# Every fourth one-hot test of a list goes from VectorE to GpSimd

## The chip, the cores and the metric

The kernel runs on one NeuronCore of one Trainium2 chip. The metric is the device time of one execution in microseconds. Three runs of the kernel before gave 2284.84, 2287.78 and 2289.15 us; the median is 2287.78 us.

The core's engines are called by the profile PE (TensorE matmul), PEld (TensorE weight load), DVE (VectorE), ACT (ScalarE), POOL (GpSimd) and SP (SyncE, which here only issues DMAs).

## The reference

Four graph-attention layers run one after the other on 4096 nodes with 256 features each, over one adjacency matrix `adj` (4096 x 4096, int32) that all four share. It is sparse: about one entry in 256 is set, and the diagonal is always set. Cut to what matters:

```
for layer in 0..3:
    V  = x @ W                                   # 4, 4, 2, 1 heads
    e[i, j]  = leaky_relu(s1[i] + s2[j])         # per head
    att = softmax over j of (e where adj[i, j] else -inf)
    out = att @ V           # layer 3: also a negative attention, then fc and elu
    x = layernorm(x + out)
```

Because so few entries of a row of `adj` are set, 128 rows of it together touch only about four in ten of the columns. The kernel makes use of this.

## The kernel before

**Lists.** The 4096 nodes are 32 tiles of 128. For each tile `m` of 128 target nodes, the kernel makes a list of the source nodes that any of the 128 targets is connected to. It has room for 13 x 128 entries beside the tile's own 128 nodes, 14 positions of 128 in all. With the list goes a packed mask `cm` of 128 targets by 14 x 128 entries, and `idx`, the node numbers of the entries. `lists` (L288) is a generator with 36 steps. Its `prepare` (L370) reads a part of `adj` by DMA (`raw`, 512 KB each, L378), turns it into bytes on ACT (`mk`, L380) and finds on DVE which source nodes are hit (L384). `places` (L389) computes with matmuls the place of each hit node in its list. `pack` (L422) does the packing for one tile `m`.

**The one-hot tests.** `pack` goes through the 31 other source tiles `j` in order. For each it knows at build time a window of 1, 2 or 3 positions into which the nodes of tile `j` can fall. One instruction, L436, compares a row of numbers (`iota`, float16) with the place of each of the 128 source nodes (a [128, 1] operand), and leaves a one-hot matrix `oh` (bfloat16, 128 x 128, 256 or 384). One matmul for each position of the window (L442) then multiplies it with the bytes of the adjacency tile and adds the product into a PSUM bank. When the last tile that touches a bank is done, ACT copies the bank to `cm` (L449). At the end `cm` is stored to memory (L450) and `idx` is computed on DVE (L453 to L455). Over all 32 lists there are 992 tests and 2336 matmuls of L442. The buffers of `oh` come from a pool of 8.

```
oh = ohp.tile([P, WMAX], BF16, name="oh")
nc.vector.tensor_scalar(oh[:, :n * P], iota[:, :n * P], self.place[:, it, j:j + 1], None,
                        op0=ALU.is_equal)
```

**A layer.** For each row tile, `RowTile.load` (L619) gathers the rows of V and of the score terms of the listed nodes from memory: 13 indirect DMAs that GpSimd issues (L634), and one plain DMA for the tile's own nodes (L631). They land in slots `G`, two positions to a slot in layers 0 to 2. Layer 0 has 16 slots, and a row tile needs 7. `half` (L638) does seven of the 14 positions at a time: ACT computes exp(S + d) for three heads (L687, 128 x 128 each); for the fourth head DVE multiplies exponentials (L678, L682); DVE masks each head's 128 x 896 weights (L684 and L688); PE multiplies the weights with the gathered values (L696; L699 in layers 2 and 3). In layers 0 and 1 the mask is first copied into PSUM (L653), so that L684 and L688 read one input from SBUF and one from PSUM.

**Stages and order.** `run` (L482) mixes the lists into layer 0. First the projections of layer 0 run together with the first 14 steps of `lists`. Then in layer 0's loop over row tiles, `part(m, 0)` issues the gathers of tile m + 1 and the first half of tile m, the next step of `lists` (tile m + 10, `LEAD`) follows, and then `part(m, 1)`:

```
for m in range(NT):
    layer.part(m, 0)
    if m + LEAD < NT:
        next(lists)
    layer.part(m, 1)
```

The instructions are not left in this order: a scheduler of the framework reorders them when the program is built, by this order as priority and by its own estimate of when each can run. What it decides is fixed: on the chip each engine works through its own queue in order. In the profile the tests of L436 run from 57.6 to 663.0 us. Layers 1 to 3 use the lists without any further test. In those, L938 (with L927, L928, L935) treats the last row tiles of layers 2 and 3 without a list.

Of the kernel before, what the change touches and what calls it, by code (L numbers as in the profile page):

```python
# [39 lines left out]
BF16 = mybir.dt.bfloat16  # L40
# [5 lines left out]
ALU = mybir.AluOpType  # L46
# [4 lines left out]
P = 128  # L51
# [77 lines left out]
WMAX = max(n for _, n in WINDOW.values()) * P  # L129
# [59 lines left out]
class Program:  # L189
# [98 lines left out]
    def lists(self, ctx):  # L288


        tc, nc, ins, shared = self.tc, self.nc, self.ins, self.shared

        def pool(name, bufs):
            return ctx.enter_context(tc.tile_pool(name=name, bufs=bufs))

        cst, rawp, mkp, ohp = pool("icst", 1), pool("raw", 4), pool("imk", 2), pool("oh", 8)
# [5 lines left out]
        iota = cst.tile([P, WMAX], F16, name="iota")  # L302
# [41 lines left out]
        for j in range(NT):  # L344
            m = 0
            while m < NT:
# [6 lines left out]
                a, n = WINDOW[m, j]  # L353
# [10 lines left out]
        class Block:  # L364
# [57 lines left out]
            def pack(self, it):  # L422
                m, mk = self.blk * BT + it, self.mk
                cm = cmp_.tile([P, NP, MC], U8, name="cm")
                nc.scalar.copy(cm[:, FRONT, :], mk[:, m, it, :])
                order = [j for j in range(NT) if j != m]
                touches = {}
                for j in order:
                    a, n = WINDOW[m, j]
                    for k in range(a, a + n):  # L430
                        touches.setdefault(k // 3, []).append((j, k))
                accs = {}
                for j in order:
                    a, n = WINDOW[m, j]
                    oh = ohp.tile([P, WMAX], BF16, name="oh")
                    nc.vector.tensor_scalar(oh[:, :n * P], iota[:, :n * P], self.place[:, it, j:j + 1], None,  # L436
                                            op0=ALU.is_equal)
                    for k in range(a, a + n):
                        b, s = divmod(k, 3)
                        if b not in accs:  # L440
                            accs[b] = prog.bank(prog.pthree)
                        nc.tensor.matmul(accs[b][:, s * MC:(s + 1) * MC], oh[:, (k - a) * P:(k - a + 1) * P],  # L442
                                         mk[:, j, it, :].bitcast(FP8), start=touches[b][0] == (j, k),
                                         stop=touches[b][-1] == (j, k), skip_group_check=True)
                        if touches[b][-1] == (j, k):
                            e = min(3, NG - 3 * b)
                            got = accs[b][:, :e * MC].rearrange("p (s c) -> p s c", c=MC)
                            o = 3 * b + (3 * b >= FRONT)
                            nc.scalar.activation(cm[:, o:o + e, :], got, AF.Copy, scale=EDGE / 2.0)  # L449
                nc.sync.dma_start(out=shared["maskC"][m], in_=cm)  # L450

                t = wk.tile([P, NP], F32, name="t")
                nc.vector.scalar_tensor_tensor(t, cm[:, :, P], 16.0, cm[:, :, P + 1], op0=ALU.mult, op1=ALU.add)  # L453
                nc.vector.scalar_tensor_tensor(t, t, 16.0, cm[:, :, P + 2], op0=ALU.mult, op1=ALU.add)
                nc.vector.tensor_tensor(shared["idx"][:, m, :], t, limit, op=ALU.min)  # L455
# [1034 lines left out]
```

## Time and profile before

| | |
|---|---|
| median of 3 runs | 2287.78 us |
| the profiled execution, its own time | 2288.18 us |
| its span, first to last instruction | 2286.4 us |
| granted TensorE clock, mean | 0.961 |
| busy: PE, PEld, DVE, ACT, POOL | 2026.1, 1835.8, 1798.3, 1741.5, 1493.2 us |
| one-hot tests, L436 | 992, from 57.6 to 663.0 us, 225.7 us busy |
| gathers on GpSimd, L634 | 1456, 1480.2 us busy |

The page gives for each engine its busy time, its share of the span and its instructions, and further down the groups of instructions by line with busy time, the mean duration of one in ns, and the idle time just before them with what ended it. Durations of neighbouring DVE instructions overlap in the records: the 992 tests have a mean of 304 ns, but together they cover only 225.7 us, 228 ns each. A table of stretches gives busy time by engine between two moments. The list of waits tells who waited for whom.

### The profile page before, as it was taken

How to read it: one execution, taken by the hardware profiler on the slowest of the kernel's cores; microseconds unless marked ns; L12 is line 12 of the kernel's file. 1: busy time of each engine (PE TensorE's matmuls, PEld its weight loads, DVE VectorE, ACT ScalarE, POOL GpSimd, SP SyncE). 2: the span in 40 equal slices, each digit the busy share in tenths (PEclk: the TensorE clock that was granted, in tenths of full speed). 3: DMA queues.
4: the chain of work that ended last, by engine and by line, in shares of the span. 5: the costliest groups of instructions: out<-in, count | busy, mean ns of one | idle time of the engine just before them, and what ended most of it. 6: DMA issues, size and time to landing. Idle time of an engine off the chain costs nothing.

```text
span 2286.4 us, 49074 instructions
## 1 busy us (share of the span) xinstructions
PE 2026.1 (89%) x15689; PEld 1835.8 (80%) x15689; DVE 1798.3 (79%) x5317; ACT 1741.5 (76%) x4977; POOL 1493.2 (65%) x1596
## 2 busy tenths in 40 slices
PE   4888888988999968998889898989998799999996
PEld 2667877877889958998888887989997688888885
DVE  2898998989999968998888895887885365566566
ACT  4778887977789958988788886988883666676664
POOL 2117664646567777777777777777761677777773
PEclk7999999999999989999999999999999899999998
DMA  8889777866456765666666666778764788888884
GB/s 279 257 262 349 219 231 250 282 201 212 143 155 188 208 181 158 190 182 165 177 170 172 176 168 176 221 213 233 217 201 139 243 268 274 270 259 282 261 255 139
DMA packets 250320, 493.00 MB, mean 216 GB/s; under 512 B 44385, under 2 KB 156610, under 8 KB 249666
## 3 DMA queue, kind: packets, MB, share of 16 engines
q0 software_dynamic: 81536, 245.30, 38.0%
q1 hardware_dynamic: 168514, 244.46, 33.5%
q8 instruction: 126, 2.06, 0.4%
q14 instruction: 144, 1.18, 0.2%
HBM read 437.05 MB, written 52.54 MB: 214 GB/s over the span
## 4 chain that ended last, share of the span: by engine, by line
PE 51%; DVE 15%; DMA 14%; ACT 11%; issue 5%; POOL 3%; SPq 0%; DVEq 0%; ACTq 0%; POOLq 0%
PE bank L699 16%; PE bank L696 14%; PE bank L938 10%; DMA G<-vals,idx 8%; ACT w L687 6%; PE bank L550 5%; PE bank L442 4%; POOL G L634 3%; DVE w L688 3%; DMA raw<-in_adjB_dram 2%; DVE w L684 2%; DVE oh L436 2%; DVE w L678 1%; DMA G<-vals 1%; ACT mk L380 1%
## 5 line engine op out<-in xcount | busy, mean ns | idle before, releaser
L634 POOL DMA_INDIRECT G<-vals,idx x1456 | 1480.2, 1017 | 754.2 <-issue 205.0
L687 ACT ACTIVATE w<-S,G 128x128 f32<-128x128 f32 x3248 | 988.2, 389 | 122.9 <-DMA G<-vals,idx 106.8
L696 PE MATMUL bank<-w,G 128*65 128x128 f32 x7168 | 842.9, 277 | 102.0 <-DVE w L684 79.0
L696 PEld LDWEIGHTS bank<-w,G 128*65 128x65 f32 x7168 | 800.6, 140 | 120.8 <-DVE w L684 91.3
L699 PE MATMUL bank<-G,w 128*128 128x257 f32 (+1 forms) x2688 | 491.3, 340 | 33.6 <-DVE w L666 11.8
L699 PEld LDWEIGHTS bank<-G,w 128*128 128x128 f32 x2688 | 431.8, 193 | 83.5 <-DVE w L666 14.7
L688 DVE SCALAR_TENSOR_TENSOR w<-w,bank 128x896 f32<-128x896 f32 x384 | 411.7, 1081 | 21.0 <-ACT w L687 20.5
L938 PE MATMUL bank<-vw,pw 128*128 128x129 f32 (+1 forms) x2048 | 301.2, 304 | 6.6 <-issue 3.2
L938 PEld LDWEIGHTS bank<-vw,pw 128*128 128x128 f32 x2048 | 276.9, 193 | 23.7 <-issue 3.7
L664 ACT ACTIVATE w<-S,G 128x128 f32<-128x128 f32 x392 | 140.0, 391 | 128.7 <-DMA G<-vals 64.3
L436 DVE TENSOR_SCALAR oh<-iota,place 128x256 bf16<-128x256 f16 (+2 forms) x992 | 225.7, 304 | 14.7 <-PE bank L442 14.1
L442 PE MATMUL bank<-mk,oh 128*128 128x132 fp8e4 x2336 | 188.5, 224 | 18.1 <-DVE oh L436 9.2
L550 PE MATMUL bank<-wext,xT 128*128 128x268 f32 (+3 forms) x640 | 181.5, 415 | 16.4 <-ACT xT L541 14.4
L678 DVE TENSOR_TENSOR w<-S,G 128x256 f32<-128x256 f32 x384 | 154.4, 418 | 51.8 <-DMA G<-vals,idx 48.9
L442 PEld LDWEIGHTS <-oh 128*128 128x128 bf16 x2336 | 144.2, 98 | 58.8 <-DVE oh L436 27.3
L380 ACT ACTIVATE mk<-raw 128x1024 uint8<-128x1024 int32 x128 | 130.7, 1053 | 25.8 <-DMA raw<-in_adjB_dram 25.7
L550 PEld LDWEIGHTS bank<-wext,xT 128*128 128x128 f32 x640 | 118.4, 203 | 35.6 <-ACT xT L541 16.9
L927 ACT ACTIVATE pw<-Sw,d 128x512 f32<-128x512 f32 x192 | 131.6, 714 | 17.0 <-PE bank L938 12.7
L935 DVE TENSOR_TENSOR pw<-pw,mw 128x512 f32<-128x512 f32 x64 | 44.0, 692 | 124.3 <-ACT pw L934 65.6
L928 DVE SCALAR_TENSOR_TENSOR pw<-pw,mw 128x512 f32<-128x512 f32 x192 | 126.9, 692 | 18.2 <-ACT pw L927 17.4
L684 DVE SCALAR_TENSOR_TENSOR w<-w,bank 128x896 f32<-128x896 f32 x128 | 138.7, 1083 | 0.9
L688 DVE SCALAR_TENSOR_TENSOR w<-w,mk 128x896 f32<-128x896 f32 x80 | 86.7, 1087 | 43.1 <-ACT w L687 42.0
(131 smaller groups left out, 1605.0 us busy)
## 6 DMA issues: line engine op xcount, KB each, us to landing
raw<-in_adjB_dram SPq DMA_DIRECT2D x128, 512.0 KB
mk<-maskC SPq DMA_DIRECT2D x112, 231.0 KB
G<-vals,idx POOLq DMA_INDIRECT x1456
S<-edge SPq DMA_DIRECT2D x64, 256.0 KB
vw<-vals SPq DMA_DIRECT2D x96, 129.0 KB
xp<-y SPq DMA_DIRECT2D x96, 128.0 KB
y<-xp SPq DMA_DIRECT2D x96, 128.0 KB
mw<-maskW SPq DMA_DIRECT2D x20, 528.0 KB
```

Source lines behind the costliest of these rows:

```text
L380: nc.scalar.activation(mk[:, q:q + 2, :, :P], src, AF.Copy, scale=EDGE)
L436: nc.vector.tensor_scalar(oh[:, :n * P], iota[:, :n * P], self.place[:, it, j:j + 1], None, op0=ALU.is_equal)
L442: nc.tensor.matmul(accs[b][:, s * MC:(s + 1) * MC], oh[:, (k - a) * P:(k - a + 1) * P], mk[:, j, it, :].bitcast(FP8), start=touches[b][0] ...
L550: nc.tensor.matmul(pp[:, :c1 - c0], self.xT[:, k, :], wext[:, k, c0:c1], start=(k == 0), stop=(k == KT - 1 and brow is None))
L634: nc.gpsimd.indirect_dma_start(out=self.place(pos), out_offset=None, in_=sh["v"][n][:NODES[t], :], in_offset=bass.IndirectOffsetOnAxis(ap= ...
L678: nc.vector.tensor_tensor(w[h][:, k:k + 2, :], S[:, h:h + 1, :].to_broadcast([P, 2, P]), dd[:, :, V + T + h:V + T + h + 1].to_broadcast([P ...
L684: nc.vector.scalar_tensor_tensor(w[h], w[h], LEAST, mh, op0=ALU.max, op1=ALU.mult)
L687: nc.scalar.activation(w[h][:, k, :], S[:, h, :], AF.Exp, bias=d(k, h))
L688: nc.vector.scalar_tensor_tensor(w[h], w[h], LEAST, mh, op0=ALU.max, op1=ALU.mult)
L696: nc.tensor.matmul(accs[0][:Wd, h * P:(h + 1) * P], v, w[h][:, k, :], **how)
L699: nc.tensor.matmul(a, w[h][:, k, :], v, **how)
L938: nc.tensor.matmul(accs[it][:, c:c + Wd], p[:, it, :], v[:, c:c + Wd], start=(j == 0 and h == heads[0]), stop=(j == NT - 1), skip_group_ch ...
```

## The change

In `pack`, every test with `j % 4 == 3` is issued on GpSimd instead of VectorE. It writes to buffers of a name of its own, `ohg`, of which there are 4. The other tests stay on VectorE with their 8 buffers. The operation, its operands and the matmuls that read the result are the same.

```diff
-                    oh = ohp.tile([P, WMAX], BF16, name="oh")
-                    nc.vector.tensor_scalar(oh[:, :n * P], iota[:, :n * P], self.place[:, it, j:j + 1], None,
-                                            op0=ALU.is_equal)
+                    side = j % 4 == 3
+                    oh = ohp.tile([P, WMAX], BF16, name="ohg" if side else "oh", bufs=4 if side else None)
+                    (nc.gpsimd if side else nc.vector).tensor_scalar(oh[:, :n * P], iota[:, :n * P],
+                                                                     self.place[:, it, j:j + 1], None, op0=ALU.is_equal)
```

## The prediction

> **What bounds the kernel now.** I read first the table of busy time by stretches, cut at the first test (57 us), at the first weights of layer 0 (175 us) and at the last test (about 665 us), then the groups by line, then the waits in the middle stretch, then the order of time.
>
> ```profile
> core 0: us, PE busy (x) PEld busy (x) DVE busy (x) ACT busy (x) POOL busy (x), PEclk, DMA share, GB/s
> 57.00:175.00 118.00, 99.77 (x956) 76.63 (x957) 104.73 (x454) 87.30 (x220) 16.35 (x17) 0.92 0.84 263
> 175.00:665.00 490.00, 428.64 (x4190) 387.84 (x4187) 457.49 (x1432) 402.02 (x1191) 290.15 (x291) 0.96 0.72 229
> ```
>
> The second stretch, lists beside layer 0, lasts 490 us for 22 row tiles: 22.3 us each. DVE is the busiest engine (457.49 of 490, 93%), PE follows (87%), POOL has 290. In the first stretch DVE (89%), PE (85%) and DMA (84%) are all near the limit and POOL is nearly idle.
>
> ```profile
> L436 DVE TENSOR_SCALAR oh<-iota,place 128x256 bf16<-128x256 f16 (+2 forms) x992 | 225.7, 304 | 14.7 <-PE bank L442 14.1
> L634 POOL DMA_INDIRECT G<-vals,idx x1456 | 1480.2, 1017 | 754.2 <-issue 205.0
> ```
>
> The tests cover 225.7 us of DVE, 0.2275 us each. By size they take 252, 296 and 321 ns for 128, 256 and 384 elements: 0.27 ns for one more element, where the masking of L688 takes 1081 ns for 896, 1.2 ns each. [...]
>
> ```profile
> POOL G L634 <- PE bank L696: 83.7, 44, 10.5
> PEld L442 <- DVE oh L436: 17.4, 39, 2.0
> PE bank L442 <- DVE oh L436: 7.1, 10, 1.7
> ```
>
> These are waits in the second stretch: who waited for whom, us, times, the longest. POOL's queue stands still 83.7 us because a slot `G` isn't free until PE has read it. PE waits little for tests.
>
> ```profile
> 409.35 4.91 DVE L436 TENSOR_SCALAR oh<-iota,place 128x384 bf16<-128x384 f16 x22
> 409.48 0.99 POOL L634 DMA_INDIRECT G<-vals,idx  x1 [0.30 <-issue]
> 410.78 1.11 POOL L634 DMA_INDIRECT G<-vals,idx  x1 [0.30 <-ACT cm L449]
> 412.20 1.10 POOL L634 DMA_INDIRECT G<-vals,idx  x1 [0.30 <-ACT cm L449]
> 413.61 0.98 POOL L634 DMA_INDIRECT G<-vals,idx  x1 [0.30 <-issue]
> ```
>
> The order of time of one row tile: most tests of a list come in one run (22 in 4.91 us), some earlier in twos to fives between other work. At the same time POOL issues a row tile's 13 gathers back to back (398.02 to 414.59 us, 16.6 us), one each 1.25 us, and stands idle some 4.5 to 10 us until the next row's slots are free. Beside the run of tests a gather takes 1.1 us instead of the usual 0.95.
>
> [...]
>
> **The change, step by step.**
>
> *Removed from DVE.* Of the 31 tiles of a list, 8 have j % 4 = 3 (7 where m is one of them): 24 x 8 + 8 x 7 = 248 tests. At 0.2275 us that is 56.4 us of DVE: of the 321 tests before 175 us a quarter, 80 tests, 18 us; of the 671 after it 168 tests, 38 us.
>
> *Added to POOL.* The windows of the moved tests come to 31 x 128, 124 x 256 and 93 x 384, a mean of 288 elements. The nearest rows are POOL's affine selects, also a compare over one input:
>
> ```profile
> L319 POOL TENSOR_SCALAR_AFFINE_SELECT tri<-ones 128x128 bf16<-128x128 bf16 x1 | 0.3, 287 | 0.0
> L325 POOL TENSOR_SCALAR_AFFINE_SELECT tot<-ones 128x4 bf16<-128x4 bf16 x1 | 0.2, 184 | 0.0
> ```
>
> That is 0.83 ns an element on 0.18 us. Lower end: 0.18 + 288 x 0.83 ns = 0.42 us. [...] I take 0.55 us. Eight a row: 4.4 us on a POOL that has 16.6 of 22.3 us occupied: 21.0 us, so it fits, though barely, and stops fitting at (22.3 - 16.6) / 8 = 0.71 us.
>
> *The lock, on DVE's side.* [...] Mean 0.345 us, against the 0.2275 us saved: a loss of 0.12 us a test, 168 x 0.12 = 20 us of DVE time. With DVE at 93% I let three quarters through: +15 us. [...]
> In the first stretch tests are most of DVE's work (84 us in all three forms)[...], a loss of 0.20 x 80 = 16 us. There half is hidden by the loading of `raw` and by PE: +8 us. [...]
>
> *The new waits.* A moved test waits for one of 4 buffers, that is for an earlier L442 on PE, and for `place`, done a block ahead. Behind it on POOL's queue are the gathers of the next row; those who wait for them are L678 on DVE and L687 on ACT. The gathers that begin at 398 us serve weights that DVE begins at 418 us (first half, whose six gathers are issued by 405) and 428 us (second half, all issued by 414.6), with some 3 us to land: about 10 us of cover on each, and 4.4 us of tests fit under it. I charge nothing; without that cover each row would lose up to 4.4 us. The other way round, a moved test stands behind gathers: PE works in order and needs test j = 19, 23, 27, 31 in the middle of the run; alternating with gathers the last four take 4 x (1.25 + 0.55) = 7.2 us instead of the 4.91 us of the run. Behind the waiting L442 stand L696 and the projections. The list is ten row tiles ahead and the scheduler can put other matmuls between, so I charge a tenth of 2.3 x 22 us: +5 us, with 0 and +50 as ends. Nothing moves on SP, and no DMA is added or taken away.
>
> Sum: +15 + 8 + 5 = +28 us against the profiled execution's 2288.18 us (span 2286.4; 0.4 us over the median of the runs): 2316 us.
>
> **The rivals.**
>
> *Faster: the offload simply works.* POOL makes its tests in its idle time under maskings, the lock costs next to nothing, and DVE loses 38 us in the second stretch, from 457 to 419. Then PE (429) is late next: with the 32 us now left over DVE's busy time the stretch is 429 + 32 = 461 us, -29 us; in the first stretch the way from 105 to PE's 100 gives -5 us. 2254 us. For it: DVE is the busiest, POOL has a fourth to spare, the maskings are long. Against it: lock and run. It decides at a mean lock cost of 0.2275 us a test. With a half-way lock the gain is 5 to 20 us. Chance of any gain over 0.2%: 0.29.
>
> *Same.* The lock gives back what the move saved, and lists are ahead enough for the rest: 2288 us. Chance 0.11.
>
> *Slower by far: POOL becomes the bound.* If a test takes 1 us, POOL needs 16.6 + 8 = 24.6 us a row, 2.3 us over the period; after the first 10 us of cover this is 2.3 x 22 - 10 = +41 us[...]: about 2288 + 75 = 2363 us. Chance 0.15.
>
> That the change doesn't do what it says isn't likely: the diff leaves no other engine to take the tests.
>
> **How the numbers follow.** My forecast, a moderate loss of some 5 to 55 us, has 0.45; POOL-bound 0.15; same 0.11; gain 0.29. About 0.2% (4.6 us) is what a measurement of this kernel can tell from no change. So slower 0.60, same 0.11, faster 0.29. The range: the low end of 2260 us leaves out only the fullest form of the gain (about one in ten), the high end of 2372 us the worst of the POOL-bound case (one in ten). The likeliest case alone reaches from 2293 to 2343 us.
>
> **What would show it.** L436 on DVE with 744 tests and on POOL with 248; [...]DVE's remaining tests and L678 longer, or with gaps, where POOL has a test; DVE's busy and idle time together in the second stretch not down by 38 us; waits of PE L442 for POOL above DVE's 24 us of before; after 700 us nothing changed. The prediction is wrong if the second stretch gets shorter than 485 us, or if POOL's tests last over 0.71 us and gathers become what ends ACT's and DVE's waits there.

## The result, and the profile after

The changed kernel takes 2427.14 us (median of 4 runs, 2424.33 to 2429.73) against 2288.47 us of the kernel before, measured beside it: a ratio of 1.0612, 95% interval 1.0591 to 1.0632, or +139 us. The forecast was 2316 us with a range up to 2372 us: the sign was right, the size was not. The lines of code stand one lower than before: the test is L437, its matmul L443, the gather L635, the weighted matmul L697.

First the table of stretches of the changed kernel, cut at the same times as before, with one stretch more because the last test now ends at 797.5 us:

```profile
core 0: us, PE busy (x) PEld busy (x) DVE busy (x) ACT busy (x) POOL busy (x), PEclk, DMA share, GB/s
...
57.00:175.00 118.00, 93.97 (x871) 69.39 (x871) 97.94 (x341) 76.75 (x192) 86.53 (x84) 0.87 0.70 221
175.00:665.00 490.00, 352.26 (x3292) 334.95 (x3293) 349.01 (x989) 328.81 (x951) 375.37 (x372) 0.85 0.62 203
665.00:800.00 135.00, 101.22 (x979) 97.81 (x978) 101.57 (x307) 82.52 (x269) 99.88 (x101) 0.88 0.46 135
```

In the 490 us in the middle DVE is now busy for 349 where it was 457, and PE for 352 where it was 429. POOL comes nearest to its limit: it is busy for 375, and about 0.3 us pass ahead of each of the 237 gathers in it, so some 446 of the 490 us are taken. Yet it isn't full either. The last test ends 134.5 us later than before (797.5 against 663.0), and from there to the end the kernel takes 1630 us where it took 1623. The loss lies where the lists are made.

The costliest groups, from the page of the changed kernel:

```profile
L635 POOL DMA_INDIRECT G<-vals,idx x1456 | 1486.0, 1021 | 559.9 <-issue 211.1
...
L437 POOL TENSOR_SCALAR ohg<-iota,place 128x256 bf16<-128x256 f16 (+2 forms) x248 | 252.4, 1031 | 75.6 <-DVE place L411 59.5
...
L437 DVE TENSOR_SCALAR oh<-iota,place 128x256 bf16<-128x256 f16 (+2 forms) x744 | 197.3, 339 | 77.6 <-PE bank L443 77.1
...
L443 PE MATMUL bank<-mk,ohg 128*128 128x132 fp8e4 x558 | 87.5, 252 | 165.3 <-POOL ohg L437 164.5
```

The counts are those of the forecast, 248 and 744. A test on POOL takes 1.03 us, almost twice what was assumed. The last line is the one to look at: ahead of the matmuls that use POOL's tests PE stood idle for 165 us, and POOL is named as the cause. The waits from 175 to 800 us, with total, times and longest in us, say the same, and one thing more:

```profile
PEld L443 <- POOL ohg L437: 167.0, 37, 14.2
PE bank L443 <- POOL ohg L437: 159.2, 33, 14.0
DVE oh L437 <- PE bank L443: 72.4, 14, 11.0
...
POOL G L635 <- PE bank L697: 33.3, 39, 3.7
```

PE waits for POOL, about 5 us at a time (159.2 us in 33 waits); DVE waits for PE, which has to read a test before its buffer is free (72.4 us); and POOL waits for PE (33.3 us). (Of POOL's 39 waits for L697 most are the 0.3 us that pass ahead of any gather, and ten are 2 us or more.) Two engines that wait for each other are the sign of a loop. The order of time shows it (start, duration, engine, line; in brackets idle time before and who ended it):

```profile
473.77 1.22 POOL L635 DMA_INDIRECT G<-vals,idx  x1 [0.16 <-ACT w L688]
...
489.02 0.63 PE L443 MATMUL bank<-mk,oh 128*128 128x132 fp8e4 x8
...
493.20 0.94 POOL L635 DMA_INDIRECT G<-vals,idx  x1 [0.30 <-issue]
494.17 8.19 POOL L437 TENSOR_SCALAR ohg<-iota,place 128x384 bf16<-128x384 f16 x8
...
495.50 0.51 PE L443 MATMUL bank<-mk,ohg 128*128 128x132 fp8e4 x3 [5.85 <-POOL ohg L437]
...
498.78 7.38 PE L697 MATMUL bank<-w,G 128*65 128x128 f32 x56
...
505.13 1.03 POOL L635 DMA_INDIRECT G<-vals,idx  x1 [2.77 <-PE bank L697]
```

POOL issues 15 gathers here, two more than a row has (473.77 to 494.14 us, 20.4 us with one test among them). Only then comes its run of 8 tests: the last four of one list and the first four of the next, since there are four buffers. PE is done with what it has at 489.65 and stands until the first of these tests is there (495.50, 5.85 us). Behind that matmul on PE's queue stands the next half of L697. The first of its masked weights were there at 486.79 (end of L685), 2.9 us before PE stood still, and yet it starts only at 498.78, after the last of L443: PE keeps to the order of its queue. It is this half that frees the slots `G`, and POOL's next gathers wait for that until 505.13. From gather burst to gather burst that is 20.4 + 1.3 (one test) + 3.3 (the rest of the list) + 6.4 (into L697) = 31.4 us for 15 gathers. POOL itself is taken up for 28.6 of them and stands still for the last 2.8. On average, between 300 and 600 us, POOL issues 141 gathers, 27.7 us for 13; in the kernel before it issued 167, 23.4 us for 13. So two things are in the longer row: the tests on POOL take time of their own, and POOL and PE wait for each other.

### The profile page after: what moved, and what is told of

Same layout as the page of the kernel before. It is cut to its first block, busy times and chain, and to the rows that moved or that the text cites. A ratio compares the mean times of both kernels' runs of the same rounds, so it can differ in the third digit from the quotient of the medians.

```text
span 2427.9 us, 49044 instructions
## 1 busy us (share of the span) xinstructions
PE 2059.6 (85%) x15689; PEld 1887.7 (78%) x15689; DVE 1782.3 (73%) x5069; ACT 1738.8 (72%) x4977; POOL 1751.4 (72%) x1844
## 3 DMA queue, kind: packets, MB, share of 16 engines
q0 software_dynamic: 81536, 245.30, 35.3%
## 5 line engine op out<-in xcount | busy, mean ns | idle before, releaser
L635 POOL DMA_INDIRECT G<-vals,idx x1456 | 1486.0, 1021 | 559.9 <-issue 211.1
L697 PE MATMUL bank<-w,G 128*65 128x128 f32 x7168 | 846.9, 280 | 60.9 <-DVE w L685 48.1
L697 PEld LDWEIGHTS bank<-w,G 128*65 128x65 f32 x7168 | 817.9, 143 | 72.3 <-DVE w L685 57.0
L689 DVE SCALAR_TENSOR_TENSOR w<-w,bank 128x896 f32<-128x896 f32 x384 | 409.1, 1078 | 20.5 <-ACT w L688 20.0
L437 POOL TENSOR_SCALAR ohg<-iota,place 128x256 bf16<-128x256 f16 (+2 forms) x248 | 252.4, 1031 | 75.6 <-DVE place L411 59.5
L437 DVE TENSOR_SCALAR oh<-iota,place 128x256 bf16<-128x256 f16 (+2 forms) x744 | 197.3, 339 | 77.6 <-PE bank L443 77.1
L443 PE MATMUL bank<-mk,ohg 128*128 128x132 fp8e4 x558 | 87.5, 252 | 165.3 <-POOL ohg L437 164.5
L450 ACT ACTIVATE cm<-bank 128x396 uint8<-128x396 f32 (+1 forms) x160 | 68.7, 451 | 210.8 <-PE bank L443 210.8
L443 PE MATMUL bank<-mk,oh 128*128 128x132 fp8e4 x1778 | 184.6, 248 | 13.1 <-DVE oh L437 11.1
L679 DVE TENSOR_TENSOR w<-S,G 128x256 f32<-128x256 f32 x384 | 157.4, 426 | 49.9 <-DMA G<-vals,idx 47.9
L443 PEld LDWEIGHTS <-ohg 128*128 128x128 bf16 x558 | 48.0, 111 | 173.9 <-POOL ohg L437 173.5
L443 PEld LDWEIGHTS <-oh 128*128 128x128 bf16 x1778 | 138.1, 112 | 32.4 <-DVE oh L437 24.1
```

What stands on the lines that cost most here:

```text
L437: (nc.gpsimd if side else nc.vector).tensor_scalar(oh[:, :n * P], iota[:, :n * P], self.place[:, it, j:j + 1], None, op0=ALU.is_equal)
L635: nc.gpsimd.indirect_dma_start(out=self.place(pos), out_offset=None, in_=sh["v"][n][:NODES[t], :], in_offset=bass.IndirectOffsetOnAxis(ap= ...
L679: nc.vector.tensor_tensor(w[h][:, k:k + 2, :], S[:, h:h + 1, :].to_broadcast([P, 2, P]), dd[:, :, V + T + h:V + T + h + 1].to_broadcast([P ...
L689: nc.vector.scalar_tensor_tensor(w[h], w[h], LEAST, mh, op0=ALU.max, op1=ALU.mult)
L697: nc.tensor.matmul(accs[0][:Wd, h * P:(h + 1) * P], v, w[h][:, k, :], **how)
```

## The experiments

**Theory A, the loop**: POOL's tests stand behind the gathers, PE's matmuls behind the tests, the gathers behind PE's matmuls. **Theory B, POOL's own time**: 13 gathers and 8 tests of 1.03 us don't fit into 22.3 us. **Theory C, the slowing** (the recorded texts say "lock"): DVE's tests get longer while POOL has a test. By what means they would, no run shows. The three were taken apart one by one.

**Eight buffers instead of four (e1_bufs8).** All 8 tests of a list can then be made ahead of the gathers.

```
-oh = ohp.tile([P, WMAX], BF16, name="ohg" if side else "oh", bufs=4 if side else None)
+oh = ohp.tile([P, WMAX], BF16, name="ohg" if side else "oh", bufs=8 if side else None)
```

> The change with 8 ohg buffers in place of 4, so that GpSimd can make all tests of a list one row tile ahead. Theory A, queue order (PE stands because the last four tests of a list lie behind the 13 gathers of the next row tile, and only four fit ahead): PE's 164 us of waits for ohg fall below 40 us and the time comes back to 2290 to 2320 us. Theory B, GpSimd's own time (16.6 us of gathers and 8.2 us of tests against a row of 22.3 us): whatever the order, a row lasts 24.8 us or more, so the time stays at 2340 us or above, and the waits move to the gathers. Theory C[...]: no difference from the change as it is, 2427 us.

Measured: 2364.1 us, ratio to before 1.0321 (1.0292 to 1.0350); 63 us less than the changed kernel. That fits B (2340 us or more), not A alone (2290 to 2320 us). POOL's own order of time in this run:

```profile
474.79 8.92 POOL L437 TENSOR_SCALAR ohg<-iota,place 128x256 bf16<-128x256 f16 x8
483.87 1.03 POOL L635 DMA_INDIRECT G<-vals,idx  x1 [0.17 <-PE bank L443]
...
499.98 0.95 POOL L635 DMA_INDIRECT G<-vals,idx  x1 [0.30 <-issue]
500.96 8.53 POOL L437 TENSOR_SCALAR ohg<-iota,place 128x256 bf16<-128x256 f16 x8
```

From run to run of tests it is 26.2 us: 8.9 us of tests and 17.1 us of 13 gathers (25.3 us on average between 300 and 600 us). From 175 to 740 us POOL pauses for longer than the 0.3 us ahead of a gather only once (1.2 us). The loop is gone and POOL sets the pace: B. PE still waits for POOL, now the slowest engine (from 175 to 730 us):

```profile
PE bank L443 <- POOL ohg L437: 66.1, 46, 9.0
```

**The moved tests left out (e4_leave_out).** What is the relief of DVE worth without any cost? The kernel makes no test where j % 4 = 3, and their matmuls read one tile of zeros, so the lists lack those nodes.

```
+if j % 4 == 3:
+    oh = none
+else:
     oh = ohp.tile([P, WMAX], BF16, name="oh")
     nc.vector.tensor_scalar(oh[:, :n * P], ...)
```

> The 248 tests with j % 4 = 3 are left out altogether (their matmuls read one tile of zeros, so the entries of these source tiles are missing from the lists); GpSimd makes none. This is what the relief of VectorE is worth if GpSimd cost nothing. If VectorE sets the pace of the list stage: 56 us of its time gone, 34 us or more off, about 2254 us. If PE, the gathers or the loads set it as much: 2270 to 2288 us.

Measured: 2232.35 us, ratio 0.9743 (0.9713 to 0.9773), -58 us for 248 tests of 0.2275 us, which are 56.4 us. DVE's time counts in full. PE, at 429 of the 490 us from 175 to 665 us before, does 458 in this run (granted clock 0.99 there, 0.96 before), so it does not hold DVE's relief back. The gathers move as many bytes as before (245.30 MB), so lighter transfers are not the cause. The group of DVE's tests:

```profile
L441 DVE TENSOR_SCALAR oh<-iota,place 128x256 bf16<-128x256 f16 (+2 forms) x744 | 174.8, 301 | 7.1 <-PE bank L447 6.6
```

**Room on POOL (e6_plain_change, and e7_plain_before as its control).** In layer 0, eight of a row's 13 gathers are made plain copies of some rows by SP, in the changed kernel and in the kernel before alike. They bring other rows than the list names. POOL then has ample time for tests, and no long burst stands ahead of them; what is left is relief and slowing.

```
     ...
+    if n == 0 and t % 3:
+        nc.sync.dma_start(out=self.place(pos), in_=sh["v"][n][t * P:(t + 1) * P, :])
+        continue
     ...
```

> The change, with 8 of the 13 gathers of each row tile of layer 0 replaced by plain copies of 128 rows in order, issued by SP (same bytes, other rows, so layer 0's values differ): GpSimd's row falls to 5 gathers and 8 tests, 6.3 + 8.2 = 14.5 us, far under any row. To be held against e7, which has the same copies without the change. Theory that queue order and GpSimd's time are all there is: the difference to e7 is the worth of the relief found by leaving the tests out, -58 us. [...](0.2 to 0.35 us of VectorE for each test on GpSimd, as the longer tests of e1 and e3 suggest): 50 to 85 us of VectorE come back, difference -10 to +30 us.

> The kernel before with the same 8 gathers of a row tile of layer 0 as plain copies on SP: the control for e6. GpSimd was not what set the pace of the kernel before, so all theories expect little in the list stage, and some gain after it, where ACT waits for gathers of layer 0: 2250 to 2290 us.

Measured: e6 2253.82 us, ratio 0.9846 (0.9828 to 0.9863); e7 2260.13 us, ratio 0.9877 (0.9860 to 0.9894). Without loop and without a full POOL the change gains 6 us by the medians, and since the intervals just overlap it may be nothing (the two profiled executions, 2262.62 and 2256.52 us, differ the other way). DVE's tests, in the control and then in the changed version:

```profile
L436 DVE TENSOR_SCALAR oh<-iota,place 128x256 bf16<-128x256 f16 (+2 forms) x992 | 221.5, 293 | 8.9 <-PE bank L442 8.9
```

```profile
L437 DVE TENSOR_SCALAR oh<-iota,place 128x256 bf16<-128x256 f16 (+2 forms) x744 | 221.4, 372 | 3.3 <-PE bank L443 3.2
```

This pair is theory C in two lines: 744 tests beside POOL's take DVE as long as all 992 did alone. Each test on POOL costs DVE (221.4 - 744 x 0.2233) / 248 = 0.22 us, as much as it takes off. The last tests end at 647 and 645 us. In the changed version PE waits for POOL's tests for less than 3 us in all.

**The tests twice (e3_extra).** The kernel before, with the 248 tests made once more on POOL into four buffers that nobody reads.

```
 nc.vector.tensor_scalar(oh[:, :n * P], ...)
+if j % 4 == 3:
+    more = ohp.tile([P, WMAX], BF16, name="ohg", bufs=4)
+    nc.gpsimd.tensor_scalar(more[:, :n * P], ...)
```

> All 992 tests on VectorE as before; GpSimd makes the 248 tests once more into 4 buffers that nobody reads. [...] Theory A: 2290 to 2300 us. Theory B: GpSimd's row of 24.8 us makes the gathers late, 2330 to 2360 us, with ACT and VectorE waiting for G in the list stage. Theory C: VectorE's tests and two-input operations get longer by some 30 us in all, about 2310 to 2320 us, without more waits for G.

Measured: 2360.87 us, ratio 1.0308 (1.0278 to 1.0337). It was meant to measure the slowing alone and doesn't: as nothing waits for these tests the scheduler bunches them (25 in a row, 27 us), and gathers behind them come late (DVE's L682 waits 11.8 us for `G`). What it gives on the slowing is that DVE's 992 tests take 278.5 us instead of 225.7: 0.21 us for each test on POOL. How much of the 70 us is slowing and how much late gathers, it doesn't tell. It does show what the slowing is like. In the 27 us in which POOL makes 25 tests without a pause, DVE does this:

```profile
437.99 27.08 POOL L440 TENSOR_SCALAR ohg<-iota,place 128x256 bf16<-128x256 f16 x25 [1.31 <-DVE place L411]
...
455.39 1.08 DVE L682 TENSOR_TENSOR w<-S,G 128x256 f32<-128x256 f32 x3
...
457.79 6.88 DVE L436 TENSOR_SCALAR oh<-iota,place 128x384 bf16<-128x384 f16 x22
```

In the kernel before, a run of 22 tests took 4.91 us (at 409 us), and the three multiplications of L682 took 1.09 us (L678, at 407 us), against 1.08 here. So DVE's tests go on beside POOL's, 0.3 us longer for each test of POOL (6.88 - 4.91 us over 6.4 tests of 1.08 us), and the multiplications aren't held up here.

**Half as many tests (e5_eighth, e8_small).** Every eighth test (j % 8 = 7, 124 in all), or the four with the smallest windows at the ends of a list (j = 0, 3, 28, 31; 124, mean 0.83 us), each with four buffers, enough for a list.

```
-side = j % 4 == 3
+side = j % 8 == 7            # e5_eighth
+side = j in (0, 3, 28, 31)   # e8_small
```

> Only every eighth test (j % 8 = 7, 4 a list) goes to GpSimd, with 4 buffers: a whole list's share fits ahead, and GpSimd's row is 16.6 + 4.1 = 20.7 us, under 22.3 us. Theory A and theory B: no wait of PE for ohg to speak of, 2275 to 2290 us. Theory C: half of the lock stays against half of the relief, 2295 us or more.

> Four tests a list on GpSimd as in e5, but those with the smallest windows (j = 0, 3, 28, 31: 62 of 128 and 62 of 256 elements, mean 192 where e5 has 288). By the durations found (0.61 us for 128, 0.95 us for 256) a test costs GpSimd 0.78 us instead of 1.06[...]. Theory of the lock and theory of GpSimd's time: faster than e5, 2255 to 2272 us. If the last two of a list then come late behind the gathers: 2280 to 2300 us.

Measured: e5 2278.2 us, ratio 0.9943 (0.9919 to 0.9967); e8 2276.83 us, 0.9951 (0.9934 to 0.9968). Both are faster than before by about half a per cent; e8 lies between its two expectations. Four tests of 1.07 us and 16.6 us of gathers are 20.9 us, under the 22.3 us of a row; the four buffers hold a whole list; and PE waits for POOL's tests only 7.5 us (e5) and 25.6 us (e8). DVE's 868 tests take 219.3 and 210.0 us; the slowing takes back 0.18 us a test in e5 and 0.10 in e8.

**Short tests (e9_narrow, e10b).** The moved tests are cut to 128 columns, and all matmuls of the window read those; what stood in columns 128 to 383 is left out. With four buffers (e9_narrow) and with eight (e10b).

```
+c = P if side else n * P
-(nc.gpsimd if side else nc.vector).tensor_scalar(oh[:, :n * P], iota[:, :n * P],
+(nc.gpsimd if side else nc.vector).tensor_scalar(oh[:, :c], iota[:, :c],
...
-    nc.tensor.matmul(accs[b][...], oh[:, (k - a) * P:(k - a + 1) * P],
+    nc.tensor.matmul(accs[b][...], oh[:, :P] if side else oh[:, (k - a) * P:(k - a + 1) * P],
```

> The change with every test on GpSimd cut to 128 elements (the matmuls of a moved tile all read these 128 columns; columns 128 to 383 of its one-hot are left out). A test then takes about 0.61 us, near the 0.55 us that the prediction put in, and GpSimd's row is 16.6 + 4.9 = 21.5 us. If the price of a test was the only thing wrong: about 2316 us as forecast. If the order of GpSimd's queue is the greater part (the last four tests behind the 13 gathers, with GpSimd's time now under the row): PE still waits over 60 us for ohg, 2345 us or more. If both the price and the lock scale with the length and the order hardly costs: 2270 to 2300 us.

> The kernel of e10 again (moved tests cut to 128 elements, columns 128 to 383 left out, and 8 buffers), on a chip where the kernel before takes some 2290 us. GpSimd's own time the rest of e1: 2250 to 2275 us. The place of the tests among the gathers: 2300 us or more.

Measured: e9 2401.33 us, ratio 1.0488 (1.0469 to 1.0506); e10b 2285.25 us, 0.9985 (0.9974 to 0.9995). A test falls to 0.63 us, and POOL's row with it to 16.6 + 5.0 = 21.6 us, which fits. With four buffers most of the loss stays all the same, 112 of 139 us. The waits of e9 from 175 to 800 us:

```profile
PEld L444 <- POOL ohg L438: 145.2, 31, 11.5
PE bank L444 <- POOL ohg L438: 139.1, 31, 11.3
POOL G L636 <- PE bank L698: 65.0, 41, 5.7
```

PE waits for POOL while POOL has 65 us of idle time waiting for PE: the loop without a full engine in it. Eight buffers take 116 us off. Then POOL again works without a pause, here over two rows of e10b (11 gathers in the first, 15 in the second; the view ends at 520 us, inside the last line's run):

```profile
473.45 4.55 POOL L438 TENSOR_SCALAR ohg<-iota,place 128x128 bf16<-128x128 f16 x7
...
491.92 5.25 POOL L438 TENSOR_SCALAR ohg<-iota,place 128x128 bf16<-128x128 f16 x8
...
516.78 3.68 POOL L438 TENSOR_SCALAR ohg<-iota,place 128x128 bf16<-128x128 f16 x6
```

The two rows together take 43.3 us, 21.7 each. DVE's 744 tests take 191.9 us in e10b, 17 us more than in e4, so the slowing is small for short tests (0.07 us each). The run was expected at 2250 to 2275 us, or at 2300 or more, and is neither; that POOL, this full, leaves nothing to gain is the likely reason, not a tested one.

**The best version (e11b).** The four small windows of e8 with eight buffers.

```
-side = j % 4 == 3
+side = j in (0, 3, 28, 31)   # and bufs=8
```

> The kernel of e11 again (four tests a list with the smallest windows, 8 buffers). Loop through the buffers still costing in e8: 2255 to 2268 us. Lock and relief balanced, or another cause: 2270 to 2285 us. On the other chip it was equal to the kernel before (ratio 1.0004), which speaks for the second.

Measured: 2273.96 us, ratio 0.9937 (0.9916 to 0.9959), against 0.9951 (0.9934 to 0.9968) with four buffers: no difference that can be told. It has the lowest median of the versions that make every test and gather, though e5 and e8 can't be told from it. PE's waits for POOL's tests are 19 us in six pieces.

**The first ten lists alone (e12b).** `side` only where m < `LEAD`. These lists are made mostly ahead of layer 0, where POOL has few gathers: neither loop nor a full POOL.

```
-side = j % 4 == 3
+side = j % 4 == 3 and m < LEAD
```

> The kernel of e12 again (only lists 0 to 9 give every fourth test to GpSimd). Lock against relief: 2280 to 2292 us. No lock: 2270 us. On the other chip it was 0.6% slower, so above 2295 us would say that the early lists lose more than the lock.

Measured: 2307.58 us, ratio 1.0083 (1.0058 to 1.0108), +20 us. Here the slowing can be seen with the eye. DVE's and POOL's tests side by side:

```profile
71.65 6.67 DVE L437 TENSOR_SCALAR oh<-iota,place 128x384 bf16<-128x384 f16 x22
71.94 7.49 POOL L437 TENSOR_SCALAR ohg<-iota,place 128x384 bf16<-128x384 f16 x7 [0.51 <-PE bank L443]
```

A run of 22 tests took 4.91 us on DVE before (at 409 us); beside seven tests on POOL it takes 6.67. Over the kernel DVE's 914 tests take 229.6 us instead of 207.9 at 0.2275 us each: 21.7 us for 78 moved tests, 0.28 us each, where 0.2275 was saved. That is a net 4 us. The other 16 us of the loss are not explained by it, so the early lists lose more than the slowing, as the expectation says for a time above 2295 us. Nearly all of it is lost before layer 0's rows: their first masking of weights (L685) starts 16 us later than before, and from there to the end the distance hardly grows. The granted clock from 57 to 175 us was 0.86 here and 0.92 before, but whether that is cause or effect of engines standing still, no run here tells.

**Where each version loses and gains.** Each half of a row tile has one masking L684 (L685 in the changed kernel). Its start in the first half of a row tile of layer 0 tells how far a version is behind the kernel before at that point (us; a minus is ahead):

| | row tile 5 | row tile 25 |
|---|---|---|
| the changed kernel | +50 | +134 |
| e1_bufs8 | +35 | +67 |
| e5_eighth | +12 | -11 |
| e11b | +10 | -20 |
| e12b | +17 | +17 |
| e4_leave_out | -6 | -58 |

Every version here with tests on POOL comes to row tile 5 late, e1 and the changed kernel most of all. In the next 20 row tiles e5 and e11b win 23 and 29 us, and e4, with twice the tests and no cost, 52. Not all of that is DVE's relief: after 185 us its tests take only 7 (e5) and 12 us (e11b) less than before. Why the start loses so much and the rows win so much stays open, and a version that moves tests from the eleventh list on was not run.

**On other chips.** e6 to e9 ran on a second chip, where the kernel before takes 2288.88 us, as good as on the first (2290.64 and 2287.79 us beside the other runs). The kernels of e10b, e11b and e12b also ran on a third (as e10, e11 and e12), where the kernel before takes 2794.42 us. There PE stands idle 198 us ahead of L697 for nothing that the profile shows (e12's kernel, granted clock 0.89), and the ratios are 0.991 (0.9882 to 0.9937), 1.0004 (0.9988 to 1.0020) and 1.0058 (1.0036 to 1.0079). They aren't used above.

**The sum.** Taken in this order, by differences: relief of DVE -58 us (e4); the slowing +52 us (the -6 us of e6 against e7, less the relief); POOL's own time +80 us (e1 at +74 us, where e6 against e7 is at -6); the loop +63 us (the changed kernel less e1). That these make +137 of the +139 us is no test of them, since each begins where the one before ends; and the slowing's share takes for granted that the relief would be worth 58 us with the plain copies too. POOL's share is what is left: 2.5 us a row (24.8 less 22.3) over 22 rows are an estimated 55 us, and the slowing, stronger in e1 than in e6 (0.32 against 0.22 us a test, 25 us for 248), can be the rest. The parts don't add up in any order. The loop alone, with short tests, is 116 us (e9 less e10b), since a loop hides a full engine beside it: shortening the tests alone gains 26 us, more buffers alone 63, both together 142.

## Why the prediction was right and wrong

The direction was right. Two steps failed, about equally large: the price of a test on POOL, and with it "it fits, though barely"; and the new waits, charged at +5 us.

*Removed from DVE*: right, 248 tests and 56.4 us. That PE "is late next" was wrong in the faster rival: DVE's time counted one for one (-58 us in e4, not -34).

*Added to POOL*: the first step that failed; the term was mis-sized. Its row was the affine select, 0.83 ns an element on 0.18 us (287 ns for 128, 184 for 4), which makes 0.42 us; the 0.55 us taken above that were the author's estimate, which no trace showed. Measured, by size, in the changed kernel:

```profile
L437 POOL TENSOR_SCALAR ohg<-iota,place 128x384 bf16<-128x384 f16 x93 | 118.9, 1282 | 8.0 <-PE bank L443 7.3
...
L437 POOL TENSOR_SCALAR ohg<-iota,place 128x128 bf16<-128x128 f16 x31 | 18.9, 610 | 0.2
```

That is (1282 - 610) / 256 = 2.6 ns an element on 0.27 us, three times the select's time. With it POOL needs 16.6 + 8.2 = 24.8 us a row, not 21.0, and "it fits, though barely" falls by the text's own bound of 0.71 us. What was charged at nothing is worth +80 us in the sum above. This is the rival "POOL becomes the bound", put at 2363 us and 0.15; e1_bufs8, where the loop is gone and relief and slowing nearly cancel, took 2364. That the two figures meet is luck: of its +75 us the rival had +41 from POOL's time, where that came to +80, and the rest from the slowing, which less the relief came to -6. Its chance was too low. The estimate of a cost that the trace didn't show started from an instruction of another kind, and too much was built on it.

*The lock, on DVE's side*: right in that DVE's tests get longer, somewhat high. The prediction took 0.345 us a test in the second stretch and 0.43 in the first; these were the author's estimates, and no trace of the kernel before showed a loss of that kind. Measured over the whole kernel were 0.22 (e6), 0.21 (e3), 0.18 (e5), 0.28 in the first ten lists (e12b) and 0.32 (e1). In the changed kernel itself it is only (197.3 - 174.8) / 248 = 0.09 us; DVE is busy for only 349 of 490 us there (457 before), but whether that is the reason no run tells. So the balance with the relief is about -6 us where +15 and +8 were charged. The tests were slowed, not stopped: DVE made 22 in 6.88 us, against 4.91 before, beside tests of POOL that follow each other without a gap (e3). And L678, which the prediction also expected to get longer, didn't in the change against its control (416 and 415 ns a piece, e6 and e7).

*The new waits*: the second step that failed. It charged "a tenth of 2.3 x 22 us: +5 us, with 0 and +50 as ends". Measured: 159 us in which PE stood still for POOL's tests, and a loop worth +63 us, or +116 with short tests, by the runs that take it away. The prediction did name each link: the tests behind the gathers, L696 behind the waiting L442, POOL's 83.7 us of waiting for slots `G`. But it priced them one at a time. Gathers behind tests it put at nothing. Tests behind gathers it put at 2.3 us a row, as if the two alternated, where the whole run of tests came behind 13 to 15 gathers and PE stood 5.85 us in the turn shown; and it let a tenth of that through, on the ground that "the scheduler can put other matmuls between". It never closed the circle: what stands behind the waiting matmul is just what frees the slots for the gathers that the test stands behind. While the circle is closed, a row lasts as long as the way around: 27.7 us on average, where POOL alone needs 24.8. Nor did it count that four buffers hold half a list: the second half of the tests cannot start before the first half is used, and so falls behind the gathers.

*Gathers' cover of 10 us*: held. (Its 3 us for a gather to land are at the low end: the chain of the kernel before has five gathers from 175 to 700 us, of 2.8 to 5.6 us.) In the changed kernel L679 waits for `G` 3.5 us in all from 175 to 800 us, so of the second sign of being wrong only half came: the tests lasted over 0.71 us, but it was PE, not the gathers, that ended most of the others' waits (ACT's L450 stood 192.5 us for it). *Nothing after 700 us*: right but for the shift, +7 us after the last test.

## What to carry to other kernels

Before moving work to another engine's in-order queue (PE here stood 5.85 us at one test, with masked weights ready behind it), draw the circle: what stands ahead of it there, what that waits for, and whether that stands behind the work's own consumer. If it does, the way around can become the period, and the buffers must hold a whole unit of the work (here 8, a list) so that it can be made one turn ahead; then add up the receiving queue's time per period, with a price measured on that engine for that very operation. From DVE to GpSimd, count also what DVE's remaining work loses beside it: here each moved test cost DVE's own tests 0.22 us and so took back nearly all of the 0.2233 us that it saved (e6, a fourth of the tests moved), and a small share of short tests was worth 0.6% (e11b).

## What was new about the hardware

A test by is_equal on GpSimd (float16 to bfloat16, with a [128, 1] operand) takes 0.61, 0.95 and 1.28 us for 128, 256 and 384 elements a partition (the changed kernel); DVE takes 0.25, 0.30 and 0.32 (the kernel before). Where DVE makes such tests beside it, each one on GpSimd costs DVE some 0.2 to 0.3 us (0.18 in e5, 0.21 in e3, 0.22 in e6, 0.28 in e12b, 0.32 in e1), so that in e6 DVE's time for a list is the same whether it makes all tests or three quarters; tests of 128 elements cost it 0.07 us (e10b). DVE went on while GpSimd began such a test every 1.08 us: 22 tests in 6.88 us instead of 4.91 (e3). And the kernel before took 2288 us on one chip and 2794 us on another, where PE stood idle 198 us ahead of L697 for nothing that the profile shows (e12's kernel).
